# The lead-in of an attention and expert kernel: half stacks first, stores and loads on other queues

## The chip, the cores and the metric

The kernel runs on one core of one Trainium2 chip. A time is the device time of one execution in microseconds; three executions of the kernel before gave 2398.78, 2402.26 and 2404.74 us. The profile comes from another execution, which took 2406.82 us.

The core has five engines: TensorE (PE; its weight loads are PEld), VectorE (DVE), ScalarE (ACT), GpSimd (POOL) and SyncE (SP). SyncE does no arithmetic here; it issues transfers. Transfers issued by any engine are carried by 16 DMA engines. Each engine works through its own list of instructions in order and waits on semaphores for the others.

## The reference, cut to what matters

The input x has 2 batches of 2048 tokens of 256 numbers. The first half of the reference is attention with 16 heads of 16 numbers each:

```python
qkv = x @ qkv_w + qkv_b
qkv = qkv.reshape(b, s, HEADS, 3 * HEAD_DIM).transpose(0, 2, 1, 3)
q, k, v = jnp.split(qkv, 3, axis=-1)
q = rot(q)   # a rotation that depends on the head, not on the token
k = rot(k)
scores = jnp.einsum('bhqd,bhkd->bhqk', q, k) / HEAD_DIM ** 0.5
attn = jax.nn.softmax(scores.astype(jnp.float32), axis=-1)
out = jnp.einsum('bhqk,bhkd->bhqd', attn, v)
out = out.transpose(0, 2, 1, 3).reshape(b, s, HEADS * HEAD_DIM)
return out @ out_w + out_b
```

A layer norm follows, then a block with two more norms, a mixing product, a router that picks two of eight experts for each token, the experts (256 to 1024 to 256 with silu), and a last norm.

## The kernel before, in words

**Stages.** The kernel first prepares (the lead-in), then runs 32 visits of attention, and then the experts on gathered lists of tokens. A visit is one batch, one block of 512 queries and one group of four heads, against all 2048 keys. Each visit has 16 steps, one for each 128 keys. A step makes four scores products (L470), adds the negated maxima by four more products (L479), takes exponentials (L485, ScalarE, eight buffers named `ex`), and multiplies them with the values (L500).

**Maxima ahead.** The maxima of the scores are found 20 steps ahead, by two half steps a step: `maxima` makes two products (L426) and two reductions on VectorE (L434). So before the first real step there are 20 steps with maxima only: 16 for visit 0 and 4 for visit 1. Visit 0 goes through its keys block by block: its first eight half steps need only the first 512 keys. These 20 steps, and what must come before them, are the lead-in.

**Stacks.** q and k are kept in two parts, a high one (the upper bits) and a low one (the rest)[...]. `prep_qk` makes one half (eight heads; `hh` is 0 or 1) of q (`s` = 0) or k (`s` = 1) for 512 tokens: two products (L345), the bias on ScalarE (`full`, L352), the high part on VectorE (`hi`, L354), and the low part on GpSimd (L358, written over `full`). Then four transfers of 256 KB issued by GpSimd (L362) store the parts to DRAM as a stack of 8 heads x 4 parts x 16 x 512. `load_stack` (L388) reads two heads of such a stack back as 128 rows of 512. `load_q` and `load_k` call it for a visit; a visit's keys are eight such loads, its queries two. `full` and `hi` have two buffers each in the pool `early`.

**Order.** The order on TensorE, ScalarE, VectorE and SyncE within the main loops is written out by hand. A list of due times (`later`, `work`) adds small pieces of other work to the steps: at most about one unit of cost a step. Before the loops the framework's scheduler places the instructions, and GpSimd's order is left to it everywhere. In the lead-in, `bank` takes its PSUM tiles from the four buffers of the scores.

**The lead-in of before.** SyncE loads x for four blocks of tokens; ScalarE's queue loads the qkv weights. VectorE rotates the weights (L266 to L268) and the bias (L238 to L248). The bias goes to DRAM and back by three small SyncE transfers (L251, L253), to change from a padded layout of heads to a dense one. For each block, x is turned (L333, L336) and the first half of k is made; for block 0 also the first half of q. Then SyncE loads visit 0 and visit 1. In the first five of the 20 maxima steps a second half (`hh` = 1) of k or q is made, one a step; in the next eight a v piece of two key tiles (`prep_v`, L371, L378), one a step.

Of the kernel before, what the change touches and what calls it, by code (L numbers as in the profile page):

```python
# [35 lines left out]
G = 4  # L36
# [27 lines left out]
def seq_postln_kernel(  # L64
# [88 lines left out]
    with ExitStack() as actx:  # L153
# [31 lines left out]
        def load_x(b, tb):  # L185
            n = b * TPB + tb

            pool, tag, bufs = (ap_, f"km{tb % 2}", 3) if b == 0 else (ep, "x_in", 1)
            x_in[b, tb] = pool.tile([P, 4, D], F32, name=f"x_in_{n}", tag=tag, bufs=bufs)
            nc.sync.dma_start(out=x_in[b, tb], in_=xv[n])  # L190

        with tc.tile_pool(name="wraw", bufs=1) as wp:
            wr = bp.tile([P, 2, H, 3, HD], F32, name="wr", tag="zx", bufs=1)
            cs = wp.tile([P, 2, H, 8], F32, name="cs")
            load_x(0, 0)
            nc.scalar.dma_start(
                out=wr.rearrange("p c h t d -> p c (h t d)"),
                in_=qkv_w.rearrange("(c p) n -> p c n", p=P),
            )
            nc.sync.dma_start(out=cols_sb, in_=cols)  # L200
            nc.sync.dma_start(out=cst_sb, in_=cst)
            nc.scalar.dma_start(
                out=cs.rearrange("p a h d -> p (a h d)"), in_=rope.partition_broadcast(P)
            )
            load_x(0, 1)
            load_x(0, 2)
            load_x(0, 3)
            for i in range(2):
                nc.gpsimd.memset(mt[i], 0.0)
            make_values()  # L210
            nc.gpsimd.memset(none, 0.0)
            nc.gpsimd.iota(none_i, pattern=[[0, 1]], base=B * S, channel_multiplier=1)
            nc.gpsimd.tensor_copy(none[:, D : D + 1].bitcast(I32), none_i)
            nc.gpsimd.memset(tri, 1.0)
            nc.gpsimd.affine_select(
                out=tri,
                in_=tri,
                pattern=[[1, P]],
                compare_op=ALU.is_gt,
                fill=0.0,  # L220
                base=0,
                channel_multiplier=-1,
            )
            nc.gpsimd.memset(ones, 1.0)
            nc.gpsimd.iota(order_i, pattern=[[1, NTILE]], base=0, channel_multiplier=0)
            nc.gpsimd.tensor_copy(order, order_i)
            nc.gpsimd.tensor_scalar_mul(base, order[:, 0:E], float(ROOM))
            after_i = bp.tile([P, E, NAFTER], I32, name="after_i", tag="after_i", bufs=1)
            nc.gpsimd.iota(after_i, pattern=[[ROOM, E], [P, NAFTER]], base=0, channel_multiplier=1)
            nc.gpsimd.tensor_copy(after, after_i)  # L230
            nc.gpsimd.iota(tok, pattern=[[P, NTB * 4]], base=0, channel_multiplier=1)
            nc.gpsimd.memset(seen, 0.0)


            t3 = wp.tile([P, 2, G], F32, name="t3")
            t4 = wp.tile([P, 2, G], F32, name="t4")
            for s in range(2):
                nc.vector.tensor_mul(  # L238
                    t3[:, s],
                    cols_sb[:, COL_BQK + 4 * s : COL_BQK + 4 * s + 4],  # L240
                    cst_sb[:, CST_COS : CST_COS + 4],
                )
                nc.vector.tensor_mul(
                    t4[:, s],
                    cols_sb[:, COL_BSW + 4 * s : COL_BSW + 4 * s + 4],
                    cst_sb[:, CST_SIN : CST_SIN + 4],
                )
            nc.vector.tensor_add(t3, t3, t4)  # L248
            with nc.allow_non_contiguous_dma(reason="the bias, from padded heads to dense ones"):
                bias = dp.tile([P, 2, 2, 2], F32, name="bias")  # L250
                nc.sync.dma_start(out=bias.rearrange("p s hh gl -> p (s hh gl)"), in_=t3)  # L251
                for gl in range(2):
                    nc.sync.dma_start(  # L253
                        out=bqk[64 * gl : 64 * gl + 64].rearrange("p s hh -> p (s hh)"),
                        in_=bias.rearrange("(j r) s hh gl -> j r (s hh) gl", r=32)[:, 0:HD, :, gl],
                    )
            for c in range(2):
                for s in range(2):
                    u1, u2 = wr[:, c, :, s, 0:8], wr[:, c, :, s, 8:16]
                    for dst, a, b_, op in (  # L260
                        (wqk[:, c, s, :, 0:8], u1, u2, ALU.subtract),
                        (wqk[:, c, s, :, 8:16], u2, u1, ALU.add),
                    ):
# [4 lines left out]
                        nc.vector.tensor_tensor(dst, t1, t2, op)  # L268
                nc.vector.tensor_copy(wv[:, c], wr[:, c, :, 2, :])

            for p in range(2):
                t5 = wp.tile([P, 1], F32, name="t5", tag="t5", bufs=2)
                nc.vector.tensor_add(
                    t5, ident[:, 2 * p : 2 * p + 1], ident[:, 2 * p + 1 : 2 * p + 2]
                )
                for at in (64 + 2 * p, 65 + 2 * p):
                    nc.vector.tensor_add(t5, t5, ident[:, at : at + 1])
                nc.vector.tensor_copy(sel[p], t5.to_broadcast([P, P]))
# [56 lines left out]
                )  # L335
            nc.scalar.copy(xT[b, tb][:, c, :], ps)  # L336

        def prep_qk(b, tb, s, hh):

            full, hi = (  # L340
                ep.tile([P, 512], F32, name=k, tag=k, bufs=2) for k in ("full", "hi")
            )
            ps = bank("ps_qk", 512)
            for c in range(2):
# [7 lines left out]
            nc.scalar.activation(full, ps, AF.Identity, bias=bqk[:, s, hh : hh + 1])  # L352

            nc.vector.tensor_single_scalar(  # L354
                hi.bitcast(I32), full.bitcast(I32), HIGH, ALU.bitwise_and
            )
            lo = full
            nc.gpsimd.tensor_sub(lo, full, hi)  # L358
            name = f"st_{b}_{tb}_{s}_{hh}"
            t = dp.tile([8, 4, HD, 512], F32, name=name, tag=name)  # L360
            for r, part in enumerate((hi, lo, hi, lo) if s == 0 else (hi, hi, lo, lo)):
                nc.gpsimd.dma_start(out=t[:, r], in_=part)  # L362
            stack[b, tb, s, hh] = t

        def prep_v(b, kt):

            ps = bank("ps_v", 2, D)
            for i in range(2):
                k = kt % 4 + i
                for c in range(2):  # L370
                    nc.tensor.matmul(  # L371
# [4 lines left out]
                        stop=(c == 1),  # L376
                    )
            nc.scalar.copy(  # L378
                vt[b][:, kt : kt + 2, 0 : 17 * H].rearrange("p k (h c) -> p k h c", c=17)[
                    :, :, :, 0:HD  # L380
                ],
                ps.rearrange("p k (h d) -> p k h d", d=HD),
# [2 lines left out]
        def load_stack(dst, b, tb, s, g, pair):  # L385

            at = 4 * (g % 2) + 2 * pair
            nc.sync.dma_start(  # L388
                out=dst.bitcast(F32),
                in_=stack[b, tb, s, g // 2][at : at + 2].rearrange("h r d s -> (h r d) s"),  # L390
            )
# [624 lines left out]
        def v_items(b, tb):  # L1016
            return [(prep_v, 2.0, b, kt) for kt in range(4 * tb, 4 * tb + 4, 2)]

        for tb in range(TPB):
            for c in range(2):  # L1020
                prep_x(0, tb, c)
            if tb == 0:
                prep_qk(0, 0, 0, 0)
            prep_qk(0, tb, 1, 0)
            if tb == 0:
                load_q(0)
        load_k(0)
        load_q(1)
        load_k(1)

        make_values()

        now[0] = -AHEAD
        for tb in range(TPB):
            later(0, lambda tb=tb: prep_qk(0, tb, 1, 1), 1.0)
        later(0, lambda: prep_qk(0, 0, 0, 1), 1.0)
        for tb in range(TPB):
            for fn, cost, *args in v_items(0, tb):
                later(4, lambda fn=fn, args=args: fn(*args), 1.0)
        now[0] = 0  # L1040
        at = 12
        for tb in range(1, TPB):
# [21 lines left out]
        with tc.manual_schedule(engines={ET.PE, ET.Activation, ET.DVE, ET.SP}):  # L1064
            for t in range(AHEAD):
                now[0] = t - AHEAD
                for half in range(2):
                    max_step(t, half)
                work(1.0)
            leading[0] = False  # L1070
            before = None
# [259 lines left out]
```

## Time and profile before

| what | value |
|---|---|
| three executions | 2398.78, 2402.26, 2404.74 us; median 2402.26 |
| the profiled execution | 2406.82 us, its span 2405.1 us |
| TensorE busy | 2277.9 us, 95% of the span |
| VectorE, ScalarE, GpSimd busy | 1534.9, 1374.4, 512.7 us |
| first x turned | 8.32 us |
| first q stored, first packet | 20.64 us |
| first maxima product | 42.15 us |
| first v piece | 78.66 us |
| first scores product, the end of the lead-in | 123.69 us |
| end of the attention steps | about 1640 us |

The span runs from the first to the last instruction of the profiled execution. A row of the timeline gives the start, the time, the engine, the line, the operation, the tile written and the tiles read, and in brackets how long the engine had been idle and what ended that. A mean over the whole span hides the lead-in, because it is 5% of it; so it is read by stretches of its own.

### The profile page before, as it was taken

What the parts mean: (1) busy time and instruction counts of PE and PEld (TensorE: products, weight loads), DVE (VectorE), ACT (ScalarE), POOL (GpSimd) and SP (SyncE); (2) the same over time, 40 slices, a digit from 0 to 9 for tenths busy, and PEclk for the clock granted to TensorE, in tenths of its full rate; (3) what the DMA queues carried; (4) which work ended last, traced back from release to release, by engine and by line L of the source; (5) the groups of instructions that cost most, each with busy time, mean ns of one, the idle gap of its engine ahead of it and who ended that gap; (6) DMA issues with size and microseconds to landing.
All of it is one profiled execution on the core that took longest, in us unless ns stands there. A gap on an engine that the chain in (4) does not pass through costs nothing.

```text
span 2405.1 us, 39739 instructions
## 1 busy us (share of the span) xinstructions
PE 2277.9 (95%) x14270; PEld 1363.8 (57%) x14270; DVE 1534.9 (64%) x3060; ACT 1374.4 (57%) x2722; POOL 512.7 (21%) x863
## 2 busy tenths in 40 slices
PE   5899999999999999999999999999998899999993
PEld 2444555545545555555555555555547788888883
DVE  2678778868877887888888888888825111111113
ACT  1167667757766776777777667777773222223333
POOL 6212221140123022011211202202122322222113
PEclk7799999999999999999999999999999899999997
DMA  7516541141124211111311211221045466567994
GB/s 217 153 42 182 144 115 54 54 132 53 53 72 123 87 55 58 58 45 54 115 45 54 71 45 53 89 71 53 1 138 168 142 193 180 176 182 225 291 292 151
DMA packets 175516, 269.69 MB, mean 112 GB/s; under 512 B 29776, under 2 KB 109656, under 8 KB 175320
## 3 DMA queue, kind: packets, MB, share of 16 engines
q1 hardware_dynamic: 142648, 213.26, 25.9%
q0 software_dynamic: 32256, 52.98, 10.1%
q8 instruction: 113, 1.85, 0.3%
q10 hardware_dynamic: 416, 0.92, 0.1%
q14 instruction: 83, 0.68, 0.1%
HBM read 204.29 MB, written 62.74 MB: 111 GB/s over the span
## 4 chain that ended last, share of the span: by engine, by line
PE 77%; DVE 16%; DMA 3%; ACT 2%; issue 1%; POOL 1%; another core or an unknown queue 0%; SPq 0%; ACTq 0%; DVEq 0%; POOLq 0%
PE av L500 19%; PE ps_mx L426 13%; DVE pm L434 12%; PE ps_h L1161 11%; PE ps_y L1176 10%; PE ps_sc L470 6%; PE ps_sc L479 6%; PE ps_qk L345 2%; DMA st<-full 2%; PE ps_v L371 1%; PE ps_p L561 1%; PE ps_mix L561 1%; PE ps_m L458 1%; PE ps_o L522 1%; PE ps_b L766 1%
## 5 line engine op out<-in xcount | busy, mean ns | idle before, releaser
L434 DVE TENSOR_REDUCE pm<-ps_mx 128x1 f32<-128x512 f32 x2048 | 1273.2, 682 | 218.3 <-PE ps_mx L426 209.3
L485 ACT ACTIVATE ex<-ps_sc 128x512 f32<-128x512 f32 x2048 | 1058.1, 603 | 453.7 <-PE ps_sc L479 433.7
L426 PE MATMUL ps_mx<-km,qm 64*128 64x512 f32 x2048 | 580.5, 474 | 36.4 <-DMA km<-st 15.3
L426 PEld LDWEIGHTS ps_mx<-km,qm 64*128 64x128 f32 x2048 | 297.7, 186 | 556.2 <-DVE pm L434 357.4
L500 PE MATMUL av<-ex,vt 128*32 128x512 f32 x4096 | 547.3, 606 | 0.0
L470 PE MATMUL ps_sc<-qm,km 64*128 64x512 f32 x2048 | 435.4, 396 | 0.4 <-ACT ex L485 0.3
L479 PE MATMUL ps_sc<-mrow,sel 64*128 64x512 f32 x2048 | 428.6, 392 | 0.0
L1168 ACT ACTIVATE hT<-ps_h,b 128x256 f32<-128x256 f32 (+1 forms) x368 | 156.3, 425 | 378.3 <-PE ps_h L1161 361.9
L1161 PE MATMUL ps_h<-xT,w 128*128 128x256 f32 (+1 forms) x1472 | 282.6, 342 | 17.2 <-issue 11.0
L1161 PEld LDWEIGHTS ps_h<-xT,w 128*128 128x128 f32 x1472 | 231.6, 193 | 62.4 <-ACT hT L1168 21.7
L1176 PE MATMUL ps_y<-w,hT 128*128 128x256 f32 x1136 | 253.7, 379 | 0.0
L479 PEld LDWEIGHTS ps_sc<-mrow,sel 64*128 64x128 f32 x2048 | 216.7, 185 | 40.5
L470 PEld LDWEIGHTS ps_sc<-qm,km 64*128 64x128 f32 x2048 | 214.8, 186 | 42.0 <-ACT ex L485 18.3
L1176 PEld LDWEIGHTS ps_y<-w,hT 128*128 128x128 f32 x1136 | 212.1, 190 | 27.5 <-issue 0.7
L1140 DVE TENSOR_SCALAR xT<-ps_x,cols_sb 128x256 f32<-128x256 f32 (+1 forms) x92 | 40.2, 478 | 271.4 <-PE ps_x L1136 271.4
L1187 POOL DMA_INDIRECT acc<-y,xg x71 | 110.1, 1551 | 390.8 <-DVE y L1186 307.0
L500 PEld LDWEIGHTS av<-ex,vt 128*32 128x32 f32 x4096 | 80.9, 108 | 133.7 <-issue 132.6
L1186 DVE TENSOR_SCALAR y<-ps_y,xg 128x256 f32<-128x256 f32 x71 | 34.2, 483 | 187.8 <-PE ps_y L1176 187.6
L132 POOL TENSOR_SCALAR op_mul<-mv 128x4 f32<-128x4 f32 x18 | 4.2, 233 | 492.7 <-DVE mv L572 491.7
L358 POOL TENSOR_TENSOR full<-full,hi 128x512 f32<-128x512 f32 x32 | 40.9, 1279 | 239.5 <-DVE hi L354 239.4
L345 PE MATMUL ps_qk<-xT,wqk 128*128 128x512 f32 x128 | 73.3, 700 | 4.8 <-ACT xT L336 1.5
L857 POOL DMA_INDIRECT x_list<-zx,at_i x64 | 64.1, 1002 | 16.5 <-issue 13.6
(198 smaller groups left out, 1160.4 us busy)
## 6 DMA issues: line engine op xcount, KB each, us to landing
w<-in_w SPq DMA_DIRECT2D x92, 1024.0 KB
km<-st SPq DMA_DIRECT2D x256, 256.0 KB
st<-hi POOLq DMA_DIRECT2D x64, 256.0 KB
st<-full POOLq DMA_DIRECT2D x64, 256.0 KB
qm<-st SPq DMA_DIRECT2D x64, 256.0 KB
xg<-x_list SPq DMA_DIRECT2D x25, 258.0 KB
x_in<-in_x SPq DMA_DIRECT2D x8, 512.0 KB
xr<-in_x SPq DMA_DIRECT2D x8, 512.0 KB
```

Of the source, the lines that this page charges most:

```text
L345: nc.tensor.matmul(ps, lhsT=wqk[:, c, s, 8 * hh : 8 * hh + 8, :].rearrange("p h d -> p (h d)"), rhs=xT[b, tb][:, c, :], start=(c == 0), st ...
L426: nc.tensor.matmul(ps[j], lhsT=qm[w][pair][r, qt * P : (qt + 1) * P], rhs=km[w][pair][r, kb * 512 : (kb + 1) * 512], start=True, stop=True,)
L434: nc.vector.tensor_reduce(pm[w][:, qt, 2 * pair + j, kb : kb + 1], ps[j], AX.X, ALU.max)
L470: nc.tensor.matmul(sc[j], lhsT=km[w][pair][r, kt * P : (kt + 1) * P], rhs=qm[w][pair][r, :], start=True, stop=False,)
L479: nc.tensor.matmul(sc[j], lhsT=sel[pair][r, :], rhs=mrow[w][r, :], start=False, stop=True)
L485: nc.scalar.activation(ex, sc[j], AF.Exp, scale=0.25)
L500: nc.tensor.matmul(av[32 * h : 32 * h + 32, :], lhsT=vt[b][:, kt, at : at + 32], rhs=exs[h], start=(kt == 0), stop=(kt == 15),)
L857: ins = nc.gpsimd.indirect_dma_start(out=x_list, out_offset=bass.IndirectOffsetOnAxis(ap=at_i[:, k, i : i + 1], axis=0), in_=zx[:, k, i, : ...
L1161: nc.tensor.matmul(ps, lhsT=w1t[:, c, k * P : (k + 1) * P], rhs=xT[:, c, :], start=(c == 0), stop=(c == 1),)
L1168: nc.scalar.activation(hT[:, k, :], ps, AF.Silu, bias=b1[:, k : k + 1])
L1176: nc.tensor.matmul(ps, lhsT=hT[:, k, s * P : (s + 1) * P], rhs=w2t[:, k, :], start=(k == 0), stop=(k == NFC - 1),)
L1187: nc.gpsimd.indirect_dma_start(out=acc, out_offset=bass.IndirectOffsetOnAxis(ap=xg[:, s, D : D + 1].bitcast(I32), axis=0), in_=y, in_offse ...
```

## The change

- **Bias.** `dense` is a copy of 64 columns of the identity. Two products of it with the rotated bias take the bias from the padded layout to the dense one, through PSUM, in place of the three transfers.
- **Weights.** The rotation goes through both halves of the rows for q first, then for k; the plain copies for v come last in the program.
- **Loads of x.** Blocks 1 to 3 of batch 0 are loaded by GpSimd in place of SyncE, after two memsets that were behind them.
- **q and k in the lead-in.** `full` and `hi` take buffers of the exponentials' tiles (`ex`, eight buffers), not of their own two each. For first halves (`hh` = 0) the low part is made by VectorE, not GpSimd. All stores of the lead-in are issued by SyncE, not GpSimd. A first half is stored by heads 0 to 3 first (four transfers of 128 KB), and its heads 4 to 7 after all blocks are through; a second half is stored whole (four of 256 KB).
- **Loads of stacks in the lead-in** are issued by GpSimd, not SyncE. Afterwards SyncE issues them as before.
- **Pieces.** In place of one piece a step, each half step of the maxima takes one small piece: one of the two products of a q or k half (ten pieces; the split into high and low parts and the stores come two pieces later), then one v tile of 128 keys (16 pieces).

```diff
-            nc.sync.dma_start(out=x_in[b, tb], in_=xv[n])
+            eng = nc.gpsimd if b == 0 and tb > 0 else nc.sync
+            eng.dma_start(out=x_in[b, tb], in_=xv[n])
...
+            dense = bp.tile([P, 4, HD], F32, name="dense", tag="comb", bufs=1)
+            nc.vector.tensor_copy(dense, ident.rearrange("p (j r) -> p j r", r=32)[:, :, 0:HD])
+            dense = dense.rearrange("p j d -> p (j d)")
...
-                bias = dp.tile([P, 2, 2, 2], F32, name="bias")
-                nc.sync.dma_start(out=bias.rearrange("p s hh gl -> p (s hh gl)"), in_=t3)
-                for gl in range(2):
-                    nc.sync.dma_start(
-                        out=bqk[64 * gl : 64 * gl + 64].rearrange("p s hh -> p (s hh)"),
-                        in_=bias.rearrange("(j r) s hh gl -> j r (s hh) gl", r=32)[:, 0:HD, :, gl],
-                    )
-            for c in range(2):
-                for s in range(2):
+            ps = ps_sc.tile([P, 4], F32, name="ps_bqk", tag="sc")
+            for gl in range(2):
+                nc.tensor.matmul(
+                    ps[64 * gl : 64 * gl + 64, :],
+                    lhsT=dense,
+                    rhs=t3.rearrange("p s (hh gl) -> p gl (s hh)", gl=2)[:, gl],
+                    start=True,
+                    stop=True,
+                )
+            nc.vector.tensor_copy(bqk.rearrange("p s hh -> p (s hh)"), ps)
+            for s in range(2):
+                for c in range(2):
...
-        def prep_qk(b, tb, s, hh):
+        def qk_parts(b, tb, s, hh):
+            first = leading[0]
             full, hi = (
-                ep.tile([P, 512], F32, name=k, tag=k, bufs=2) for k in ("full", "hi")
+                ap_.tile([P, 512], F32, name=k, tag="ex", bufs=8)
+                if first
+                else ep.tile([P, 512], F32, name=k, tag=k, bufs=2)
+                for k in ("full", "hi")
             )
...
+            def split():
+                nc.vector.tensor_single_scalar(
+                    hi.bitcast(I32), full.bitcast(I32), HIGH, ALU.bitwise_and
+                )
+                lo = full
+                (nc.vector if first and hh == 0 else nc.gpsimd).tensor_sub(lo, full, hi)
+                name = f"st_{b}_{tb}_{s}_{hh}"
+                t = dp.tile([8, 4, HD, 512], F32, name=name, tag=name)
+                stack[b, tb, s, hh] = t
+                parts = list(enumerate((hi, lo, hi, lo) if s == 0 else (hi, hi, lo, lo)))
+
+                def store(k):
+                    for r, part in parts:
+                        nc.sync.dma_start(
+                            out=t[4 * k : 4 * k + 4, r], in_=part[64 * k : 64 * k + 64]
+                        )
+
+                if first and hh == 0:
+                    store(0)
+                    return lambda: store(1)
+                for r, part in parts:
+                    (nc.sync if first else nc.gpsimd).dma_start(out=t[:, r], in_=part)
+
+            return lambda: product(0), lambda: product(1), split
...
-            nc.sync.dma_start(
+            (nc.gpsimd if leading[0] else nc.sync).dma_start(
                 out=dst.bitcast(F32),
                 in_=stack[b, tb, s, g // 2][at : at + 2].rearrange("h r d s -> (h r d) s"),
             )
...
+        second_halves = []
         for tb in range(TPB):
             for c in range(2):
                 prep_x(0, tb, c)
             if tb == 0:
-                prep_qk(0, 0, 0, 0)
-            prep_qk(0, tb, 1, 0)
-            if tb == 0:
-                load_q(0)
+                second_halves.append(prep_qk(0, 0, 0, 0))
+            second_halves.append(prep_qk(0, tb, 1, 0))
+        for store in second_halves:
+            store()
+        load_q(0)
         load_k(0)
...
+        def piece():
+            for item in list(soon):
+                item[0] -= 1
+                if item[0] <= 0:
+                    soon.remove(item)
+                    item[1]()
+            if not pieces:
+                return
+            item = pieces[0]
+            if item[0] == "qk":
+                _, tb, s = pieces.pop(0)
+                first, second, split = qk_parts(0, tb, s, 1)
+                pieces.insert(0, ("fn", second, split))
+                first()
+            elif item[0] == "fn":
+                _, second, split = pieces.pop(0)
+                second()
+                soon.append([2, split])
+            else:
+                prep_v(0, pieces.pop(0)[1], 1)
...
                 for half in range(2):
                     max_step(t, half)
+                    piece()
                 work(1.0)
             leading[0] = False
```

More of the change, by code (lines that the diff above doesn't have):

```diff
@@ L204, in seq_postln_kernel @@
             )
+            for i in range(2):
+                nc.gpsimd.memset(mt[i], 0.0)
             load_x(0, 1)
@@ L207, in seq_postln_kernel @@
             load_x(0, 3)
-            for i in range(2):
-                nc.gpsimd.memset(mt[i], 0.0)
             make_values()
@@ L232, in seq_postln_kernel @@
             nc.gpsimd.memset(seen, 0.0)
-            t3 = wp.tile([P, 2, G], F32, name="t3")
-            t4 = wp.tile([P, 2, G], F32, name="t4")
+            dense = bp.tile([P, 4, HD], F32, name="dense", tag="comb", bufs=1)
+            nc.vector.tensor_copy(dense, ident.rearrange("p (j r) -> p j r", r=32)[:, :, 0:HD])
+            dense = dense.rearrange("p j d -> p (j d)")
+            t3, t4 = (wp.tile([P, 2, G], F32, name=k) for k in ("t3", "t4"))
             for s in range(2):
@@ L248, in seq_postln_kernel @@
             nc.vector.tensor_add(t3, t3, t4)
-            with nc.allow_non_contiguous_dma(reason="the bias, from padded heads to dense ones"):
-                bias = dp.tile([P, 2, 2, 2], F32, name="bias")
-                nc.sync.dma_start(out=bias.rearrange("p s hh gl -> p (s hh gl)"), in_=t3)
-                for gl in range(2):
-                    nc.sync.dma_start(
-                        out=bqk[64 * gl : 64 * gl + 64].rearrange("p s hh -> p (s hh)"),
-                        in_=bias.rearrange("(j r) s hh gl -> j r (s hh) gl", r=32)[:, 0:HD, :, gl],
-                    )
-            for c in range(2):
-                for s in range(2):
+            ps = ps_sc.tile([P, 4], F32, name="ps_bqk", tag="sc")
[10 more added lines that the diff above has]
+                for c in range(2):
                     u1, u2 = wr[:, c, :, s, 0:8], wr[:, c, :, s, 8:16]
@@ L268, in seq_postln_kernel @@
                         nc.vector.tensor_tensor(dst, t1, t2, op)
+            for c in range(2):
                 nc.vector.tensor_copy(wv[:, c], wr[:, c, :, 2, :])
@@ L336, in prep_x, with product @@
             nc.scalar.copy(xT[b, tb][:, c, :], ps)
-        def prep_qk(b, tb, s, hh):
+        def qk_parts(b, tb, s, hh):
+            first = leading[0]
             full, hi = (
-                ep.tile([P, 512], F32, name=k, tag=k, bufs=2) for k in ("full", "hi")
+                ap_.tile([P, 512], F32, name=k, tag="ex", bufs=8)
+                if first
+                else ep.tile([P, 512], F32, name=k, tag=k, bufs=2)
+                for k in ("full", "hi")
             )
             ps = bank("ps_qk", 512)
-            for c in range(2):
+            def product(c):
                 nc.tensor.matmul(
@@ L351, in prep_qk, with prep_v @@
                 )
[L352 to L368, printed above, removed]
+                if c == 1:
+                    nc.scalar.activation(full, ps, AF.Identity, bias=bqk[:, s, hh : hh + 1])
+            def split():
[19 more added lines that the diff above has]
+            return lambda: product(0), lambda: product(1), split
+        def prep_qk(b, tb, s, hh):
+            for part in qk_parts(b, tb, s, hh):
+                rest = part()
+            return rest
+        def prep_v(b, kt, n=2):
+            ps = bank("ps_v", n, D)
+            for i in range(n):
                 k = kt % 4 + i
@@ L378, in prep_v @@
             nc.scalar.copy(
-                vt[b][:, kt : kt + 2, 0 : 17 * H].rearrange("p k (h c) -> p k h c", c=17)[
+                vt[b][:, kt : kt + n, 0 : 17 * H].rearrange("p k (h c) -> p k h c", c=17)[
                     :, :, :, 0:HD
@@ L1031, in seq_postln_kernel @@
         make_values()
[L1033 to L1039, printed above, removed]
+        pieces: list = []
+        for tb, s in [(tb, 1) for tb in range(TPB)] + [(0, 0)]:
+            pieces.append(("qk", tb, s))
+        for kt in range(16):
+            pieces.append(("v", kt))
+        soon: list = []
+        def piece():
[18 more added lines that the diff above has]
+                prep_v(0, pieces.pop(0)[1], 1)
         now[0] = 0
```

## The prediction

> **What bounds the kernel now.** I read the busy time by stretch first, to find the lead-in (everything before the first scores product, L470, at 123.69 us) and its limits; the columns are PE, PEld, DVE, ACT and POOL busy, granted TensorE clock, DMA share of 16 engines, GB/s.
>
> ```profile
> 20.00:42.00 22.00, 6.45 (x26) 3.23 (x24) 0.85 (x2) 3.52 (x6) 12.67 (x19) 0.72 0.88 223
> 42.00:78.66 36.66, 28.43 (x45) 9.96 (x45) 15.17 (x28) 4.12 (x6) 19.07 (x27) 0.59 0.97 285
> 78.66:88.95 10.29, 10.20 (x24) 6.33 (x24) 4.95 (x9) 1.17 (x2) 3.02 (x5) 0.56 0.87 240
> 88.95:106.88 17.93, 17.65 (x68) 11.01 (x68) 14.16 (x23) 2.93 (x5) 0.86 (x2) 1.00 0.30 77
> 106.88:123.69 16.81, 15.65 (x34) 7.05 (x33) 15.86 (x29) 1.17 (x2) 0.00 (x0) 0.64 0.00 1
> 123.69:1640.00 1516.31, 1482.76 (x10137) 773.60 (x10137) 1252.53 (x2277) 1052.69 (x2043) 282.47 (x561) 1.00 0.25 76
> ```
>
> From 20 to 79 us the transfers bind (share 0.88 to 0.97); then TensorE (10.20 of 10.29, 17.65 of 17.93 us); then VectorE's maxima (15.86 of 16.81). From 123.69 on TensorE is full and the diff leaves that code alone, so a lead-in that ends earlier or later moves the end by as much. The chain of waits says which transfers:
>
> ```profile
> 24.91 10.03 DMA st<-full
> ...
> 39.27 9.98 DMA st<-full
> ...
> 53.58 10.75 DMA st<-full
> ...
> 68.66 8.09 DMA st<-full
> 76.86 0.70 ACT full L352
> ```
>
> These are the stores of the stacks. The next q or k may overwrite `full` (two buffers) only when they have landed. The waits and the timeline give the sizes:
>
> ```profile
> ACT full L352 <- DMA st<-full: 46.7, 8, 7.3
> PE ps_mx L426 <- DMA km<-st: 15.3, 1, 15.3
> 16.23 0.69 ACT L352 ACTIVATE full<-ps_qk,bqk 128x512 f32<-128x512 f32 x1 [5.34 <-DMA bqk<-bias]
> 88.96 1.99 PE L371 MATMUL ps_v<-wv,xT 128*128 128x256 f32 x8
> 90.88 1.24 PE L426 MATMUL ps_mx<-km,qm 64*128 64x512 f32 x4
> 92.16 1.99 PE L371 MATMUL ps_v<-wv,xT 128*128 128x256 f32 x8
> ```
>
> 46.7 us of waiting for stores, 15.3 us for the first keys, 5.3 us for the bias; and a step with a v piece costs 3.2 us (88.96 to 92.16), all TensorE.
>
> **The change, part by part.**
>
> *Bias.* Out: three SyncE transfers between 9.59 and 16.11 us. In: a copy `dense`, two 4-column products and one small copy. In the built order `dense` stands 17 VectorE operations after the one at 9.20 us, at 0.20 us each (12.6), and the bias products stand first on TensorE: the turning of x waits from 8.32 to about 13.0. Then 2 us to the first product, two products at the slow clock (2.04 for one, 10.92 row): the first `full` starts near 19 instead of 16.23. After it 0.69 and a high part of 0.43 follow, and SyncE can store it near 20.2; with the 1.3 to 1.5 us from issue to first packet (GpSimd's: 19.17 to 20.64) the first packet goes at 21.5, against 20.64. The bias wait is gone, but nothing is gained.
>
> *VectorE subtracts* in the first five parts: at 0.69 us (L568's rows) for GpSimd's 1.28; VectorE is nearly idle there (0.85 of 22 us). Loads of x by GpSimd: needed at 17 us or later, landed by 13. Reordered wqk products, one-tile v pieces: the same operations, hidden. Zero for all.
>
> *Tiles in exponentials' buffers.* Eight for two, so the first four parts wait for nothing. Ten parts need twenty, so from the fifth on each still waits for a store: in the built order VectorE's last high part of the lead-in (second-half q) waits for SyncE's stores 43 and 44, and 56 of the 80 maxima stand behind it.
>
> *Stores by SyncE, half a stack each.* This decides. A half store has 64 source rows and a target of 4 x 16 x 512: its outermost count is 4. No row of the trace has such a big one, but two small SyncE transfers are of this kind. Each bias load (64 rows from 4 x 64) left five updates on its semaphore where 128-row transfers leave 16: one at 14.28, then four at 15.44 to 15.63. The 8-row load of b2 left one at 94.58, then eight. [...] The updates agree with 4 and 8; that they are the same four each time no run here shows. GpSimd's stores of 8 x 16 x 512 moved up to 366 GB/s between 19.5 and 28 us; at 4,096 bytes in 159 ns for one engine, that is 14 of the 16.
>
> [...] Store: 64 rows over 4 are 16 packets of 2,048 bytes at 84 ns (the median of SyncE's 2 KB packets between 150 and 500 us), 1.34 us; a whole store on 8 engines, 128/8 = 16 packets, the same 1.34. Bounds: 1.27 (GpSimd's 4 KB at 159 ns) and 1.7 (107 ns, the 95th percentile). A load of 256 KB by GpSimd costs each engine 4 packets of 159 ns, 0.64.
>
> [...]
> - first packet 21.5
> - 44 stores x 1.34 = 59.1
> - 18 loads that come before store 44 (4 of q, 8 of the first keys, 6 of the second) x 0.64 = 11.4, so 92.0
> - landing, and the high part of 0.43: 93.0.
> The first maxima can start near 39 (8 stores 10.7, two q loads 1.3, then issue and transfer of two key loads, some 5) instead of 42.15, but VectorE then stands at stores 20, 28, 32, 36, 40 and 44 in turn, 5 to 10 us each. SyncE's queue holds only these; GpSimd's 20 loads (0.6 us of issue each, like its stores) and its subtracts wait for the same stores, without adding. At 93.0, 28 half steps remain:
> - 14 with a v piece, at 3.2/2 = 1.6: 22.4
> - slow clock at their start: 3.9. By the row, the first two steps of before took 5.28 and 5.01 us (78.66 to 88.95), 3.9 over 2 x 3.2, with the clock at 0.56 although TensorE was 99% busy. [...]
> - 14 without, at 16.81/14 = 1.2: 16.8.
> Main part at 93.0 + 22.4 + 3.9 + 16.8 = 136.1, against 123.69: **+12.4 us**. The span goes from 2405.1 to 2417.5. The profiled execution took 2406.82 (1.7 around the span), 4.6 above the median 2402.26; on the median the forecast is **2414.7**.
>
> The last 16 stores end by 92.0 + 16 x 1.34 + 1.3 = 115, before the exponentials that take over their tiles (136): hidden; with a lead-in under 115 us they would be late next. The second-half keys are needed some 33 us into the main part: hidden.
>
> **Rivals.**
>
> *The stores spread over most engines* ([...]successive transfers take different fours). For: eight stores may be under way at once; the before's GpSimd stores did spread. Against: the five and nine updates. Then SyncE's issue binds, 0.45 us each (0.90 for two small loads at L993): the first maxima come near 31; ten half steps with a q or k product at VectorE's 1.24 + 0.43 = 1.67, 17; some 3 of waits; 16 v pieces x 1.6 = 25.6; 14 x 1.2 = 16.8. Main part at 93.4: -30.3, **2372**. It decides from the store's price: break-even is 123.69 - 43.1 (v pieces to end) - 1.0 - 21.5 - 11.4 = 46.7 us for 44 stores, 1.06 us each: faster from six engines on (64 rows x 84 ns / 1.06 = 5.1).
>
> *Four engines, but cheaper than summed*: 1.27 a store (-3.1), [...]half the loads in the gaps (-5.7): +1, **2403**, no change. For: TensorE starts earlier; against: the waits of before left the clock at half.
>
> *Four engines and dearer*: 1.7 a store adds 16 and the slow clock lasts longer: **2432**. For: the lead-in's busy engines did stretch packets; against: here twelve engines are nearly idle.
>
> **How the numbers follow.** Four engines as summed 0.55 (2407 to 2424), dearer 0.17, cheaper 0.10, spread 0.18 (2360 to 2386). This measurement tells 0.3% (7 us) from no change: slower than 2409.5 is most of the first two, 0.70; within, 0.11; faster, 0.19 (the spread case and a little). The likeliest case's own range is 2400 to 2438; that leaves out the whole spread case and tails, over 2 in 10, so the range reaches down to 2376.
>
> **What would show it.** Right: each half store's semaphore gets five updates; DMA share near 4/16 to 6/16 and some 110 to 180 GB/s from 25 to 90 us; VectorE's L372 high parts wait for `st` stores, the last until about 92; first scores at 136; the first maxima only 3 us earlier. Wrong: shares near 1, the last high part by 55, first scores near 93. If the first `full` starts before 17, the bias step is wrong. If stores take 1.34 but the last gate falls by 75, the order of waits was misread.

## The result, and the profile after

The changed kernel takes 2416.8 us (median of seven executions, 2415.4 to 2419.5) against 2402.3 us for the kernel before on the same chip (seven executions): a ratio of 1.0052, 95% interval 1.0037 to 1.0067. It is slower by 14.6 us at the median. The forecast was 2414.7 us. (The ratios here and below are the recorded estimates; the quotients of the medians differ from them by up to 0.001, here 1.0061.)

The busy time by stretch of the changed kernel, with the columns as in the prediction (PE, PEld, DVE, ACT, POOL busy, granted TensorE clock, DMA share, GB/s):

```profile
20.00:42.00 22.00, 10.91 (x42) 5.54 (x40) 4.47 (x8) 5.58 (x10) 3.01 (x6) 0.87 0.35 119
42.00:78.66 36.66, 18.03 (x29) 5.53 (x27) 11.47 (x19) 2.57 (x4) 8.98 (x14) 0.64 0.46 164
78.66:95.00 16.34, 12.64 (x25) 5.02 (x25) 7.22 (x12) 2.19 (x5) 5.62 (x7) 0.71 0.62 220
95.00:123.69 28.69, 27.90 (x92) 15.23 (x90) 20.64 (x33) 5.22 (x14) 0.39 (x1) 0.84 0.73 243
137.00:1650.00 1513.00, 1480.28 (x10115) 772.49 (x10115) 1249.28 (x2273) 1049.98 (x2037) 282.53 (x561) 0.99 0.25 76
```

From 20 to 79 us, where the transfers of the kernel before filled 0.88 to 0.97 of 16 engines, they now fill 0.35 and 0.46, and yet nothing else is busy: TensorE works 18 of 36.7 us. The main part (last row) is as full of TensorE as it was. (The attention steps do not end at about 1640 us: in the kernel before the last product with the values starts at 1796.7 us.) The chain of waits (start, us, what) names what all others wait for:

```profile
32.45 10.31 DMA st<-full
42.78 12.89 DMA st<-full
...
62.23 13.09 DMA st<-full
...
78.85 12.00 DMA st<-hi
90.95 0.69 ACT full L368
...
137.55 1.20 PE ps_sc L507 x2
```

It is the same kind of link as before, the stores, but now each is 10 to 13 us long, and the first scores product starts at 137.36 us instead of 123.69: 13.7 us later, which is nearly the whole loss. (The chain's row counts from 137.55; the same row of the kernel before counts from 123.88.) The waits and the timeline show how the stores reach the other engines:

```profile
DVE hi L372 <- DMA st<-full: 23.8, 6, 10.1
ACT full L368 <- DMA st<-hi: 46.5, 5, 23.4
67.51 0.51 DVE L372 TENSOR_SCALAR hi<-full 128x512 int32<-128x512 int32 x1 [10.14 <-DMA st<-full]
93.62 0.43 DVE L372 TENSOR_SCALAR hi<-full 128x512 int32<-128x512 int32 x1 [0.40 <-DMA st<-full]
```

The last high part starts at 93.62 us (93.0 had been worked out), just after the 44th store has landed (93.54). Last, the transfers from 24 to 64 us in 40 slices of 1 us, the busy tenths of 16 engines above and GB/s below:

```profile
DMA  2222222587322794222248822269422226932222
GB/s 86 80 74 92 98 102 100 143 268 244 111 94 100 147 375 176 104 102 102 100 119 264 318 107 104 98 162 367 170 102 107 100 102 158 404 125 98 104 102 98
```

The floor of this row is the mechanism. Where only half stores run it stands at two tenths and mostly 98 to 104 GB/s (74 to 92 in the first four slices). Four engines that each move 2,048 bytes in 84 ns (the median packet of SyncE's queue, here as in the kernel before) give 4 x 24.4 = 98 GB/s, and 4/16 is 0.25; from 73 to 77 us, for example, the share was 0.26 at 101 GB/s. The peaks to 404 GB/s (nine tenths of the engines) are GpSimd's loads, which do use the other engines. The same kernel on the same queue doubles this level where only its whole stores are left: 0.53 and 204 GB/s from 95 to 103 us.

### The profile page after: what moved, and what is told of

Its sections match the earlier page's. It is cut to its first block, busy times and chain, and to the rows that moved or that the text cites. A ratio compares the mean times of both kernels' runs of the same rounds, so it can differ in the third digit from the quotient of the medians.

```text
span 2417.8 us, 39793 instructions
## 1 busy us (share of the span) xinstructions
PE 2277.1 (94%) x14274; PEld 1362.1 (56%) x14274; DVE 1542.8 (64%) x3067; ACT 1375.6 (57%) x2730; POOL 494.0 (20%) x841
## 4 chain that ended last, share of the span: by engine, by line
PE 77%; DVE 16%; DMA 3%; ACT 2%; issue 2%; another core or an unknown queue 0%; SPq 0%; POOL 0%; ACTq 0%; DVEq 0%; POOLq 0%
PE av L537 19%; PE ps_mx L463 13%; DVE pm L471 12%; PE ps_h L1224 11%; PE ps_y L1239 10%; PE ps_sc L507 6%; PE ps_sc L516 6%; PE ps_qk L360 2%; PE ps_v L408 2%; DMA st<-full 2%; PE ps_mix L598 1%; PE ps_p L598 1%; PE ps_m L495 1%; PE ps_o L559 1%; PE ps_b L803 1%
## 5 line engine op out<-in xcount | busy, mean ns | idle before, releaser
L537 PEld LDWEIGHTS av<-ex,vt 128*32 128x32 f32 x4096 | 81.0, 108 | 134.1 <-issue 133.1
L376 POOL TENSOR_TENSOR full<-full,hi 128x512 f32<-128x512 f32 x27 | 34.7, 1286 | 197.9 <-DVE hi L372 197.8
L368 ACT ACTIVATE full<-ps_qk,bqk 128x512 f32<-128x512 f32 x32 | 22.0, 688 | 85.6 <-DMA st<-hi 46.5
```

Source lines behind the costliest of these rows:

```text
L537: nc.tensor.matmul(av[32 * h : 32 * h + 32, :], lhsT=vt[b][:, kt, at : at + 32], rhs=exs[h], start=(kt == 0), stop=(kt == 15),)
```

## The experiments

The runs were made on more than one chip: the kernel before took 2384.7 us beside the first four, 2401.8 beside the next three and 2386.6 beside the last two. So kernels of different groups are compared by their ratio to the kernel before. The times that were expected for the first four belong to a chip on which the kernel before takes 2402.3 us and are read as ratios too. In all of them "the last high part" is the start of the last `hi` of the lead-in on VectorE, and "first scores" the first scores product (93.6 and 137.4 us in the changed kernel, 123.7 before).

### Every store on 16 engines

The heads of a half and their 16 dimensions change places in the rows of `full` and `hi`, so that the store's outermost count is 16. The scores don't see the order, since q and k have the same.

```diff
-dense = bp.tile([P, 4, HD], F32, name="dense", tag="comb", bufs=1)
+dense = bp.tile([P, HD, 4], F32, name="dense", tag="comb", bufs=1)
...
+turn = wqk[:, c, s].rearrange("p h d -> p (h d)").rearrange(
+    "p (a d j) -> p a j d", a=4, j=4
+)
...
-    (wqk[:, c, s, :, 0:8], u1, u2, ALU.subtract),
-    (wqk[:, c, s, :, 8:16], u2, u1, ALU.add),
+    (turn[:, :, :, 0:8], u1, u2, ALU.subtract),
+    (turn[:, :, :, 8:16], u2, u1, ALU.add),
...
-        nc.sync.dma_start(
-            out=t[4 * k : 4 * k + 4, r], in_=part[64 * k : 64 * k + 64]
+        (nc.sync if first else nc.gpsimd).dma_start(
+            out=t[4 * k : 4 * k + 4, r].rearrange("j d s -> d j s"),
+            in_=part[64 * k : 64 * k + 64],
         )
...
-for r, part in parts:
-    (nc.sync if first else nc.gpsimd).dma_start(out=t[:, r], in_=part)
+for k in range(2):
+    store(k)
```

> The changed kernel, with the 64 partitions of a half in the order (d, j) instead of (j, d), so that the outermost size of every store's target is 16 instead of 4; in the lead-in all stores are half stores by SyncE, in the main part GpSimd makes half stores too (8 a stack instead of 4). Order of the work, queues and loads stay. Theory 1 (each half store lies on four engines, and 16 packets of 84 ns one after the other set 1.34 us a store): the store leaves 16 updates, its price falls to SyncE's issue, about 0.6 us, the last high part waits until about 55 us instead of 93.6, first scores near 95, time 2370 to 2385. Rival (SyncE's queue as such, or the order of half stacks and waits, sets the pace whatever engines are used): the last high part near 93, first scores near 137, time about 2417.

Measured: ratio 0.9947 (0.9930 to 0.9963), 2371.4 us. The last high part started at 70.1 us, first scores at 109.0. Each of the early stores left 16 updates within about 0.4 us (the first at 23.34 to 23.69) instead of one and then four. So the four engines were the cause of the loss, and the rival that blames the queue or the order falls. But the gain is smaller than expected: the last high part was to come near 55, and the expected 2370 to 2385 us are ratios of 0.987 to 0.993. One stretch and one wait of this kernel show what still held it:

```profile
42.00:78.00 36.00, 31.83 (x74) 12.17 (x72) 20.64 (x35) 4.95 (x11) 11.90 (x15) 0.74 0.72 239
ACT full L372 <- DMA st<-hi: 27.0, 4, 10.6
```

Four parts still waited for stores, 27.0 us in all (46.5 before the edit), and TensorE was busy for 31.8 of 36 us at a mean clock of 0.74; it ran at half clock from 37 to 50 and from 54 to 64 us. The ten half steps that carry a product of q or k took 31 us (35.1 to 66.1). How the loss divides between the two is not shown. A third limit appears behind the last high part. These are the transfers from 66 to 90 us (slices of 0.6 us), and an issue row of SyncE:

```profile
DMA  9971166666561666565656556565566565656899
GB/s 372 379 277 65 79 205 225 208 225 225 195 208 75 198 215 215 195 215 198 212 195 219 201 184 208 198 208 201 198 215 212 198 215 195 219 195 167 290 393 232
```

```profile
73.79 1.24 SPq L388 DMA_DIRECT2D st<-hi  x2
```

Here the issue sets the pace of the stores: 0.62 us for each 128 KB, one after the other, is 211 GB/s, and the row stands mostly at 195 to 225. With 80 half stores the queue has 50 us of issue to do.

### Half the stores, on eight engines

All parts of the lead-in are stored whole. A whole store has an outermost count of 8.

```diff
-if first and hh == 0:
-    store(0)
-    return lambda: store(1)
 for r, part in parts:
     (nc.sync if first else nc.gpsimd).dma_start(out=t[:, r], in_=part)
```

> The changed kernel without half stacks in the lead-in: every part is stored whole (8 x 16 x 512) by SyncE, 20 stores instead of 40, 20 packets of the same engines fewer. Theory 1 (1.34 us for a half store on four engines and the same 1.34 for a whole one on eight): the last high part waits for store 23 or 24 in place of 43 or 44, which is 20 stores and 27 us earlier: near 67, first scores near 110, time near 2390. Rival (SyncE's queue has a price per byte, so that a whole store costs two halves): the last high part near 93 as before the edit, time about 2417.

Measured: ratio 0.9970 (0.9958 to 0.9983), last high part at 73.9 us, first scores at 113.9. Whole stores of twice the bytes don't take twice the time. From 66 to 90 us:

```profile
DMA  9996535555555555555555555555555555555555
GB/s 362 376 430 253 82 89 184 191 191 188 181 181 205 191 195 195 191 208 201 208 198 208 198 208 198 208 201 201 208 201 208 201 208 201 208 195 212 195 212 198
```

Five tenths and 200 GB/s: 8 x 24.4 = 195. Two tenths with a count of 4, five with 8, both on SyncE's queue: on it the level follows the outermost count. Removing the half stacks alone turns the change from a loss into a small gain. That is less than expected (first scores near 110, a ratio near 0.995), because the last high part came 7 us later than the 67 us that had been summed. It did wait for the 24th store, as expected, but `full` no longer waits for stores (it waits for its products, 35.0 us in nine waits), and the chain shows another link ahead of that store:

```profile
62.13 3.18 POOL km L422 x6
...
65.85 1.16 POOL full L376
67.02 0.57 SPq L389
67.63 6.16 DMA st<-full
73.91 0.43 DVE hi L372
```

GpSimd issued six loads (62.13 to 65.31 us) before it made the low part of this half (65.85), so the 23rd store could not be issued before 67.02. The sum over stores had left out GpSimd's queue.

### Stores back to GpSimd, loads back to SyncE

```diff
-        nc.sync.dma_start(
+        nc.gpsimd.dma_start(
             out=t[4 * k : 4 * k + 4, r], in_=part[64 * k : 64 * k + 64]
...
-(nc.sync if first else nc.gpsimd).dma_start(out=t[:, r], in_=part)
+nc.gpsimd.dma_start(out=t[:, r], in_=part)
...
-(nc.gpsimd if leading[0] else nc.sync).dma_start(
+nc.sync.dma_start(
     out=dst.bitcast(F32),
```

> The changed kernel with the lead-in's stores issued by GpSimd and the loads of stacks by SyncE, as before the change; half stacks, tiles, bias products and x loads stay. The target of a half store keeps its 4 x 16 x 512. Theory 1[...]: GpSimd's stores spread over most engines, 40 issues of about 0.6 us are 24 us from 21 us on, the last high part near 50 to 55, first scores 95 to 105, time 2372 to 2388. Rival (the shape 4 x 16 x 512 is slow on every queue, or the order is what costs): last high part at 75 or later, first scores near 137, time about 2417.

Measured: ratio 1.0011 (1.0003 to 1.0018) over 20 executions, which scatter from 2380.6 to 2393.6. So the same 4 x 16 x 512 on GpSimd's queue does not cost what it costs on SyncE's, but the gain that was expected (a ratio of 0.987 to 0.994) did not come in the median. The profiled execution happens to be the fastest of the 20 (last high part 77.3, first scores 115.4). Its stores were not held to four engines at a time: the DMA share was 0.74 from 20 to 42 us and 0.85 from 42 to 78, against 0.35 and 0.46 in the changed kernel. Yet 0.74 of the engines moved 178 GB/s here and 235 in the half stores on 16 engines. Its chain also runs through GpSimd, which held a low part back by a memset (60.97 to 64.92 us). It does not show where the median execution spends 7 us more. The answer is neither that of the theory nor that of the rival; this point stays open.

### The exchange of queues alone

The kernel before, with SyncE's stores (whole) and GpSimd's loads in the lead-in, and nothing else of the change.

```diff
-nc.gpsimd.dma_start(out=t[:, r], in_=part)
+(nc.sync if leading[0] else nc.gpsimd).dma_start(out=t[:, r], in_=part)
...
-nc.sync.dma_start(
+(nc.gpsimd if leading[0] else nc.sync).dma_start(
     out=dst.bitcast(F32),
```

> The kernel before with one part of the change alone: in the lead-in SyncE stores (whole, 8 x 16 x 512) and GpSimd loads. Two buffers each for full and hi, bias by transfers, GpSimd's subtracts stay. Theory 1 (a whole store on eight engines 1.34 us; the last full part waits for store 32): 20.6 + 32 x 1.34 + 18 x 0.64 = 75, against 76.9 before, so first scores within 3 us of 123.7 and the ratio between 0.997 and 1.001: the exchange of queues alone costs nothing, the half stacks do. Rival (SyncE's queue as such is slower than GpSimd's): the last full part after 85, ratio above 1.004.

Measured: ratio 1.0012 (1.0004 to 1.0020), just above the expected range; the last `full` at 79.3 us (75 had been expected, before it was 76.9), first scores at 123.7 as before. SyncE's stores at five tenths of the engines (mostly 200 to 205 GB/s where they run alone) replace the wider spread of GpSimd's at almost no cost: from 22 to 38 us, loads included, 220 GB/s moved here and 222 in the kernel before; why the 2.4 us do not reach the first scores was not followed. It is the step from eight engines to four, by the half stacks, that costs.

### x by SyncE again

```diff
-eng = nc.gpsimd if b == 0 and tb > 0 else nc.sync
-eng.dma_start(out=x_in[b, tb], in_=xv[n])
+nc.sync.dma_start(out=x_in[b, tb], in_=xv[n])
```

> The changed kernel with the three later blocks of x loaded by SyncE again, so that GpSimd's memset of 128x4608 runs at its old place, ahead of VectorE's copies of the weights. Theory (the memset beside VectorE's copies made two of them 3.46 us instead of 0.75, and x was turned near 15.0 instead of 13.0): the copies 0.8 us again, first full part 1.5 to 2 us earlier, time 2414.5 to 2415.5. Rival (the copies are slow for another cause, or the delay is swallowed by the queue of stores): time 2416.8 as the changed kernel.

First the timeline of the changed kernel, then that of this one:

```profile
4.78 3.98 POOL L174 MEMSET vt<- 128x4608 f32 x1
6.67 3.46 DVE L277 COPY wv<-wr 128x256 f32<-128x256 f32 x2 [6.67 <-DMA wr<-in_qkv_w]
14.96 1.97 PE L341 MATMUL ps_x<-ident,x_in 128*128 128x128 f32 x8
```

```profile
2.23 3.93 POOL L174 MEMSET vt<- 128x4608 f32 x1
7.14 0.62 DVE L276 COPY wv<-wr 128x256 f32<-128x256 f32 x2 [7.14 <-DMA wr<-in_qkv_w]
13.42 1.97 PE L340 MATMUL ps_x<-ident,x_in 128*128 128x128 f32 x8
```

In the changed kernel GpSimd's three loads stand ahead of its memset, so this moved from 2.23 to 4.78 us and onto VectorE's two copies; these took 3.46 us instead of 0.62. Without the overlap x is turned at 13.4 us (13.0 had been predicted) instead of 15.0. That step is shown. Its worth is not: the first high part starts 1.8 us earlier (18.87 against 20.65), the last one at the same 93.6, so the lead was lost on the way through the queue of stores. First scores still came 4.3 us earlier (133.1), all of it behind the last high part, where TensorE's clock was free again from 95.6 us instead of about 104. The time shows none of that: the ratio, 1.0063 (1.0046 to 1.0080), cannot be told from that of the changed kernel. In the profile the rest of the kernel, from the first scores on, took 2264.9 us, against 2259.8 (half stores on 16 engines) and 2260.0 (whole stores) on the same chip; what these 5 us are is open.

### The changed kernel once more

It is unaltered, on the chip of the queue exchange and of the next kernel.

> The changed kernel unaltered, to stand on the same chip as the runs beside it. Theory 1 (the lead-in's delay is the whole loss): first scores near 137, 13 to 14 us after those of the kernel before, ratio 1.005 to 1.006 as on the first chip. Rival (part of the loss came in the main part on the first chip): another ratio with the same first scores.

Measured: ratio 1.0053 (1.0033 to 1.0072), last high part 94.3, first scores 138.2, 14.5 us after those of the kernel before. The loss is the same again, and it lies ahead of the first scores.

### Whole stores on 16 engines, x by SyncE

Half as many issues, and each store on all engines: the rows of a part are in the order (d, head) for all eight heads, so that a store's target is 16 x 8 x 512.

```diff
-(nc.sync if first else nc.gpsimd).dma_start(out=t[:, r], in_=part)
+(nc.sync if first else nc.gpsimd).dma_start(out=t[:, r].rearrange("j d s -> d j s"), in_=part)
...
+turn = wqk[:, c, s].rearrange("p h d -> p (h d)").rearrange("p (a d j) -> p a j d", a=2, j=8)
...
-    ps[64 * gl : 64 * gl + 64, :],
-    lhsT=dense,
+    ps,
+    lhsT=dense[:, gl].rearrange("p d a j -> p (d a j)"),
```

> As the kernel with spread stores, but every part stored whole (no half stacks) with its 128 partitions in the order (d, head), so that the target is 16 x 8 x 512: half as many stores, each on 16 engines; x loaded by SyncE again. Theory 1: a store is 8 packets of 84 ns, 0.67 us, no more than its issue by SyncE; the last high part waits until about 55 us, first scores 98 to 103, time 8 to 11 us below the half stores on 16 engines and 20 to 24 us below the kernel before (ratio 0.990 to 0.992). Rival (with 16 engines the sum of the transfers or TensorE at its slow clock already sets the pace, as 235 to 239 GB/s in both faster runs suggests): first scores near 108, ratio 0.994 to 0.995, as the half stores on 16 engines.

Measured: ratio 0.9895 (0.9880 to 0.9910), 2378.4 us against 2401.8; last high part at 58.9, first scores at 97.9. Both are close to what was expected. Its transfers from 23 to 39 us (slices of 0.4 us), and its stretches:

```profile
DMA  9997999999999999789999976999999999999999
GB/s 328 384 353 261 323 302 277 343 343 359 358 348 323 277 251 241 133 277 348 323 338 307 251 210 271 389 384 405 374 415 415 405 389 420 410 405 399 410 425 394
```

```profile
46.00:60.00 14.00, 13.94 (x43) 5.51 (x43) 13.42 (x25) 3.50 (x6) 7.91 (x9) 1.00 0.96 333
60.00:81.00 21.00, 20.61 (x81) 11.28 (x79) 17.03 (x28) 4.85 (x13) 1.58 (x3) 1.00 0.88 286
81.00:98.00 17.00, 15.83 (x34) 7.14 (x33) 16.27 (x30) 0.96 (x2) 0.00 (x0) 0.61 0.00 1
```

With all engines at work TensorE is full from 46 us on, at the full clock, then VectorE binds the last 17 us. Only one part still waits for a store (2.3 us). All other parts of the change are in this kernel, except the half stacks and GpSimd's loads of x. Together they come with a gain of 23 us by the medians (25 by the ratio) once the stores have their engines; what each of them, or the row order alone in the kernel before, is worth was not tried.

### The bias products behind the turning of x

```diff
-ps = ps_sc.tile([P, 4], F32, name="ps_bqk", tag="sc")
+def bias_products():
+    ps = ps_sc.tile([P, 4], F32, name="ps_bqk", tag="sc")
...
 for c in range(2):
     prep_x(0, tb, c)
 if tb == 0:
+    bias_products()
```

> The whole stores on 16 engines with x by SyncE, and the two bias products moved behind the first turning of x in TensorE's order (the tiles dense, t3 and t4 moved to another pool for it). Theory (bias products first on TensorE hold the turning of x until 13.0 to 13.5 us, which on the changed kernel gave away what the bias transfers had cost): x turned at about 8.3 us, the first full part at 16.3 to 17 instead of 19.4, first scores 2 to 3 us earlier than 97.9, time 2 to 3 us below the run beside it. Rival (the rotated weights or the copy dense end last anyway, or the start is swallowed later): first full part after 18.5, time within 1 us of it.

> The whole stores on 16 engines with x by SyncE, as before, to stand on the same chip as the run with the moved bias products. First scores near 98, ratio 0.988 to 0.991.

Measured: ratios 0.9884 (0.9868 to 0.9901) with the products moved and 0.9896 (0.9879 to 0.9912) without; medians 2359.8 (2359.1 to 2361.7) and 2361.8 (2360.9 to 2364.7). The timeline of the moved version:

```profile
8.12 1.94 PE L349 MATMUL ps_x<-ident,x_in 128*128 128x128 f32 x8 [8.12 <-DMA x_in<-in_x]
12.89 1.02 PE L259 MATMUL ps_bqk<-t,dense 128*128 128x4 f32 x4 [2.82 <-DVE t L281]
13.76 5.25 PE L368 MATMUL ps_qk<-xT,wqk 128*128 128x512 f32 x8
17.33 0.69 ACT L376 ACTIVATE full<-ps_qk,bqk 128x512 f32<-128x512 f32 x1 [6.65 <-PE ps_qk L368]
```

x is turned at 8.12 us, as expected, but the first `full` comes at 17.33 against 17.95 in the kernel beside it (first scores 94.9 and 95.1). `dense` is still copied at 12.39 us, between the weights' rotations, and the bias products now stand in front of the first product of q instead of the turning. Neither expectation holds: the profile shows 0.6 us at the first part and 0.2 at the first scores, the medians 2.0 us with ranges that overlap. It is worth little, if anything.

## Why the prediction was right

*The lead-in sets the end.* Right: first scores came 13.7 us later (12.4 had been forecast), the time rose by 14.6, and in most of the other kernels the same subtraction gives the ratio within 0.002: -9.8 us for whole stores (0.9959 by 2402.3, measured 0.9970), -14.7 for spread half stores (0.9939, measured 0.9947), -25.8 for spread whole ones (0.9893, measured 0.9895). The profiles of the run with GpSimd's stores (the fastest of its 20) and of that with x by SyncE don't follow it.

*Four engines, 1.34 us a store.* Right, and shown by the levels of two, five and nine tenths for half stores with an outermost count of 4 and whole ones with 8 and 16. From the first packet (22.4 us) to the last high part 71.2 us passed; 44 x 1.34 + 18 x 0.64 + 1.0 is 71.5. So close a fit is partly chance: with x by SyncE the same stretch took 73.0 us. That a count of 4 means four engines was the author's estimate, from the five and nine updates of small loads; the half stores left five updates too (the first store one at 22.16 us and four at 24.39 to 24.72), the whole ones nine. Whether it is the same four each time, the other transfers answer, if each update but a store's first is read as that of one engine. The early loads of stacks by GpSimd left twelve updates at once and four later (one key load at 46.93 to 47.31 and at 49.49 to 50.11 us), as if four of the engines had a queue and twelve had none. And the 44th store, a whole one, left one update at 83.0, four at 87.9 to 88.8 and four at 92.7 to 93.5, as if half of its engines stood behind the half stores and half did not.

*Bias.* The sign was right (nothing gained), the size too small: x was turned at 14.96 us, not 13.0, the first part came at 19.93 instead of near 19, and the first packet at 22.4 instead of 21.5. The mis-sized terms were "Loads of x by GpSimd" and "zero for all": the three loads pushed GpSimd's memset onto VectorE's copies. The explanation was also incomplete: with x turned first the gain was 0.6 us at most, since the rotated weights and `dense` are ready at about the same time.

*Tiles of the exponentials.* Right: six high parts waited for stores, the last at 93.62. The first maxima started at 41.3, not near 39; this did not matter, as VectorE stood at the gates afterwards.

*Behind the gate.* 26.3 us had been taken for the half steps with v and 16.8 for those without; they took 26.9 (93.62 to 120.54) and 16.8. The slow clock was taken by the row (3.9 us), which was near: TensorE was full at a clock of 0.50 from 91.7 to 103 us, with half steps of 2.73 us, and 26.9 - 22.4 = 4.5 us went that way. That this term fitted was in part luck: with x by SyncE the half steps with v took 22.3 us behind the same gate (93.58 to 115.91), so the slow clock cost nothing there. (In the forecast's case of cheaper stores, +1 us, 2.6 us stand for a shorter slow clock, a size that no trace had shown.)

*The rival with the stores on most engines* had its mechanism right for another kernel. It gave 93.4 us for first scores. Half stores on 16 engines reached 109.0: the first maxima came at 35.1 and not near 31 (SyncE's issue took about 0.6 us each and not 0.45, some 1 us for eight stores), and the ten half steps with a product took 31 us and not 20; the rival's sum had no slow clock in it. Whole stores on 16 engines reached 97.9 and 95.1: there these ten took 17.8 us (38.35 to 56.14), and only the first maxima were late. The gain of 30.3 us came out as 23 to 27.

## What to carry to other kernels

When stores are cut into smaller ones or go to SyncE's queue, look at the outermost count of both sides of each transfer before anything else: here, on SyncE's queue, targets of 4, 8 and 16 gave 100, 200 and (with loads beside them) mostly 250 to 420 GB/s, and the bias loads of the kernel before, with a 4 on the source's side, left five updates as the half stores did; a change of the rows' order was enough to pass from one to the next. A DMA share that stands at a steady fraction while everything waits for transfers was the mark of it here; a steady half was once the whole stores with a count of 8 and once the issue of many small ones. A share near one does not tell how many bytes move: it went with 223 to 285 GB/s in the kernel before and with 400 in the whole stores on 16 engines. A short instruction that is moved ahead on one engine (three issues of loads) also moves what stands behind it, and that can fall onto another engine's work.

## What was not expected of the hardware

- VectorE's two copies of 128 x 256 took 3.46 us while GpSimd cleared a tile of 128 x 4608, and 0.62 us when that had ended; the memset itself took 3.98 and 3.93 us. In the three other kernels of the first group that load x by GpSimd too, the copies took 3.06 to 3.22 us. Not every operation of VectorE suffers: in the changed kernel the rotations of the weights took 0.28 us each from 10.70 to 13.73 us, beside the second memset of that size (10.61 to 14.55), as one did at 15.15 us without it.
- The clock of TensorE did not come free after a fixed time of work. With hardly a gap it took from 91.7 to about 104 us in the changed kernel, but in the second run of the whole stores on 16 engines only from 35.7 to about 41:

```profile
36.00:38.50 2.50, 2.50 (x6) 0.63 (x4) 1.29 (x2) 0.00 (x0) 1.31 (x3) 0.50 1.04 407
38.50:41.00 2.50, 2.50 (x6) 0.67 (x6) 1.29 (x2) 0.00 (x0) 0.95 (x3) 0.54 1.05 406
41.00:44.00 3.00, 3.00 (x11) 1.00 (x10) 2.29 (x4) 0.69 (x1) 1.99 (x4) 1.00 1.05 406
```

  12 us against 5. And behind the same gate the clock of the kernel with x by SyncE (second row) was free where that of the changed kernel (first row) was not:

```profile
95.00:99.00 4.00, 4.00 (x11) 2.41 (x10) 2.31 (x4) 0.37 (x1) 0.39 (x1) 0.50 0.53 204
95.60:99.00 3.40, 3.37 (x14) 1.84 (x14) 2.58 (x4) 0.95 (x3) 0.00 (x0) 1.00 0.53 206
```

  What makes the difference no run here tells.
- The same kernel took 2402 us beside one group of runs and 2385 beside another, so that only ratios within a group mean anything at this size. In the profiles nearly all of it lies behind the attention: from the last product with the values to the end 605 to 608 us on the chips of the 2402 us, 591 to 592 on the others. Why is open.
